# Two graph-attention layers on 64 graphs: layer 1's values from seven half-size products instead of eight matmuls

## The chip, the cores and the metric

The kernel runs on one core of a Trainium2 chip. The metric is the device time of one execution in microseconds (us); the kernel before took 3634.82 us in the median of three runs (3634.51 to 3635.04). Engines are named as in the profile: PE is TensorE's matmul and PEld its weight load, DVE is VectorE, ACT is ScalarE, POOL is GpSimd, SP is SyncE, which here only issues DMAs.

## What is computed

There are 64 graphs of 256 nodes with 512 features, float32, and a 256 x 256 adjacency (bool) for each. Two layers follow each other, each as a residual on a normalised input:

```python
h = jnp.maximum(_layernorm(x, axis=-1), 0.0)
x = x + layer0(h, adj, ...)     # 8 heads of 64: cosine adjacency times softmax attention, then a graph convolution
h = jnp.maximum(_layernorm(x, axis=-1), 0.0)
x = x + layer1(h, adj, ...)
```

Layer 1 is masked attention with 4 heads of 64:

```python
q = split_heads(x @ Wq)          # Wq, Wk, Wv: 512 x 256
k = split_heads(x @ Wk)
v = split_heads(x @ Wv)
sim = jnp.einsum('bhid,bhjd->bhij', q, k) * scale
sim = jnp.where(adjacency_mask[:, None, :, :], sim, neg)
attn = jax.nn.softmax(sim, axis=-1)
out = jnp.einsum('bhij,bhjd->bhid', attn, v)
return out.transpose(0, 2, 1, 3).reshape(...) @ Wo + bo
```

The change is about `v = x @ Wv`, a product of 256 x 512 by 512 x 256 for each graph.

## The kernel before

The graphs go through a software pipeline. `period(i)` is called 63 times; in it, layer 0 of graph i ends, layer 0's projections of graph i + 1 are made, layer 1 of graph i starts (queries, keys, values) and layer 1 of graph i - 1 ends. `closing()` does the last graph. The whole runs in a manual schedule: each engine executes its instructions in the order in which the program text issues them, and semaphores are set by the tile framework where a tile is read, written or used again. So the order around the change is what `period` and `closing` write out by hand.

Most projections are made as a block product with seven instead of eight half-size products (a Strassen-like scheme). Of the left matrix (tokens by features, cut into four blocks a11, a12, a21, a22) `left_factors` (L257 to L260) makes four further factors s1 to s4 on POOL; of the weights, `load_seven` loads four blocks and `finish_seven` (L88 to L91) makes three more by differences on DVE, once. `seven_products` (L279 for features first, L274 for tokens first) is a generator: each `next` issues one step of products into PSUM banks, the copies of some of them on ACT (`u2`, `u4`, `u5`, L289 without a bias, L296 with one), and the sums on DVE that write the result (L304) or an intermediate (`uu`, L324). One bank, `z`, is written by three steps in turn, accumulating; between them DVE reads it. Several such generators run interleaved: `m` and `s` (layer 0's mapping and messages), `q` and `k` (its queries and keys), and `j`, layer 1's queries and keys in one (`queries_keys1`, with `wqk1`, where the first 256 features of the result are queries and the others keys).

Layer 1's values are not made so. `values_in` (L527) issues, for each half of the tokens, four matmuls with 128 x 128 of the normalised input `h1T` as weights and 256 columns of `Wv` moving, into one bank:

```python
nc.tensor.matmul(g.p_v[:, t, :], g.h1T[:, c, t * P:(t + 1) * P], w.wv1[:, c, :],
                 start=(c == 0), stop=(c == NKC - 1))
```

In `period` one half stands between the third and the fourth step of `j`, the other after it, and one DVE copy of 128 x 512 (L687) brings the bank to SBUF behind the `moments` (L197 to L200) of graph i + 3. In `closing` one half is split over the steps of `j` and the other comes after the scores, copied by ACT (L748).

The next period begins with layer 1's scores of this graph (L404, `sc<-qk`, weights of 64 rows), then layer 0's scores of the next (`sc<-qT,kT`), their exponentials on ACT (L411), and the masks on DVE (L418 with the edges of layer 1, L420 for layer 0), `units` (L387), and the halved sums of the masked exponentials on POOL (L424, later L460), on which the steps of `far_off` (L451, L454) depend.

PSUM is a ring of 8 banks, given out in turn (`bank`). SBUF tiles come from pools: `v`, `sms` (layer 0's head sums, written by `total`, L487) and `adb` (the complement of the adjacency as bf16, written on POOL by `edges`, L337, and read by the two transposing DMAs of L342, which make the mask of graph i + 2) have one buffer each. `gt` (a block-diagonal copy of `gcn_W`, L42 to L44) and `ident_b` are constants that live through the whole program; `gt` is used only in the first stage, where `fold` (L128) and `fold_bias` (L140) combine weights, and `ident_b` only in a general path that doesn't run with these inputs.

Of the kernel before, what the change touches and what calls it, by code (L numbers as in the profile page):

```python
# [8 lines left out]
F32 = mybir.dt.float32  # L9
BF16 = mybir.dt.bfloat16  # L10
# [19 lines left out]
class Weights:  # L30
# [4 lines left out]
    def __init__(self, nc, const, a):  # L35
        P, D, DH = 128, a["x"].shape[2], 64
        self.nc, self.const, self.a = nc, const, a
        self.ident = const.tile([P, P], F32, name="ident")
        make_identity(nc, self.ident)

        self.gt = const.tile([P, P], F32, name="gt")
        nc.vector.memset(self.gt, 0.0)  # L42
        for j in range(2):
            nc.gpsimd.dma_start(out=self.gt[j * DH:(j + 1) * DH, j * DH:(j + 1) * DH], in_=a["gcn_WT"])  # L44
        self.gb = const.tile([P, D // P], F32, name="gb")
        nc.gpsimd.dma_start(out=self.gb, in_=a["gcn_map_b"].rearrange("(c p) -> p c", p=P))
        self.ident_b = const.tile([P, P], BF16, name="ident_b")
        nc.vector.tensor_copy(self.ident_b, self.ident)
        self.below = const.tile([P, 1], F32, name="below")
        nc.vector.memset(self.below, -THRESHOLD)  # L50
        self.ones = const.tile([P, DH], F32, name="ones")
        nc.vector.memset(self.ones, 1.0)

        self.blk32 = const.tile([P, 32], F32, name="blk32")
        nc.vector.memset(self.blk32, 0.0)
        for j in range(2):
            nc.vector.memset(self.blk32[j * DH:(j + 1) * DH, j * 16:(j + 1) * 16], 1.0)

        self.two = const.tile([P, 2, 32], F32, name="two")
        nc.vector.memset(self.two, 0.0)  # L60
        for n in range(2):
            nc.vector.memset(self.two[:, n, n:n + 1], 1.0)
        self.wc = const.tile([P, 7, D // P // 2, D // 2], F32, name="wc")
        self.bc = const.tile([P, D], F32, name="bc")
# [7 lines left out]
    def load_seven(self, keys, name, queues=1):  # L72

        aps = [self.a[k] for k in (keys if isinstance(keys, tuple) else (keys, keys))]
        half = aps[0].shape[0] // 2
        t = self.const.tile([128, 7, half // 128, half], F32, name=name)
        for n, (i, j) in enumerate(self.BLOCKS):
            f = 0 if isinstance(keys, tuple) else j * half  # L80
            block = aps[j][i * half:(i + 1) * half, f:f + half]
            queue = (self.nc.sync, self.nc.scalar)[n % queues]
            queue.dma_start(out=t[:, n], in_=block.rearrange("(c p) f -> p c f", p=128))
        return t
# [21 lines left out]
    def load_rest(self):  # L106
        self.wv1 = self.load_w("Wv", "wv1")
        self.wqk1 = self.load_seven(("Wq", "Wk"), "wqk1")
# [11 lines left out]

    def fold(self, gws, bank, put, cs):

        nc, P = self.nc, 128
        NKC = self.gb.shape[1]
        for c in cs:
            p = bank(f"p_wc{c}", [P, NKC * P])
            for k in range(NKC):
                nc.tensor.matmul(p[:, k * P:(k + 1) * P], gws[k // 2][:, k % 2, c * P:(c + 1) * P], self.gt,  # L128
                                 start=True, stop=True)
            put(c, p)  # L130
# [3 lines left out]

    def fold_bias(self, gbb, bank):
        nc, P = self.nc, 128
        NKC = self.gb.shape[1]
        p = bank("p_bc", [P, NKC * P])
        for k in range(NKC):
            nc.tensor.matmul(p[:, k * P:(k + 1) * P], gbb[:, k, :], self.gt, start=True, stop=True)  # L140
        nc.scalar.copy(self.bc, p)
# [9 lines left out]
def fast_path(ctx, tc, a, w, chk, out):  # L151
# [41 lines left out]
    def moments(g, tag):  # L193
        st = small.tile([P, NT, 6], F32, tag="st", name=f"st{tag}")
        g.mv = small.tile([P, NT, 2], F32, tag="mv", name=f"mv{tag}")
# [136 lines left out]

    def edges(g):


        adb = sb1.tile([P, NT, S], BF16, tag="adb", name=f"adb{g.i}")
        nc.gpsimd.tensor_scalar(adb, g.ad, -1.0, 1.0, op0=ALU.mult, op1=ALU.add)  # L337
# [147 lines left out]
    def total(g, sm):  # L485
        g.sms = sb1.tile([P, S], F32, tag="sms", name=f"sms{g.i}")
        nc.scalar.activation(g.sms, sm, AF.Copy, accum_out=chk[:, g.i, 0:1])  # L487
# [4 lines left out]
    def sums_back(g):  # L492

        rt = bank(f"rt{g.i}", [P, NT, P])
        for t in range(NT):
            nc.tensor.transpose(rt[:, t, :], g.sms[:, t * P:(t + 1) * P], w.ident)  # L496
        r = small.tile([P, NT, 2, 4], F32, tag="r", name=f"r{g.i}", bufs=2)
        nc.vector.reciprocal(r, rt.rearrange("p t (k n) -> p t n k", n=32)[:, :, :2, :])  # L498
        rc = small.tile([P, NT, 2, 4], F32, tag="rc", name=f"rc{g.i}", bufs=2)
        nc.scalar.activation(rc, r, AF.Copy, accum_out=chk[:, g.i, 1:2])  # L500
        g.rk = small.tile([P, NT, H0], F32, tag="rk", name=f"rk{g.i}", bufs=2)
        for t in range(NT):
# [12 lines left out]
    def queries_keys1(g):  # L515

        left = left_factors(g.h1T, "sh", f"1_{g.i}")
        qk = sb1.tile([P, 2 * NIC, S], F32, tag="qk1", name=f"qk1_{g.i}")
        g.q1T, g.k1T = qk[:, :NIC, :], qk[:, NIC:, :]
        return seven_products(left, w.wqk1, None, qk, f"p_qk1{g.i}")  # L520

    def values_in(g, t, cs=range(NKC)):
        if t == 0 and cs[0] == 0:
            g.v = sb1.tile([P, NT, INNER], F32, tag="v", name=f"v{g.i}")
            g.p_v = bank(f"p_v{g.i}", [P, NT, INNER])
        for c in cs:
            nc.tensor.matmul(g.p_v[:, t, :], g.h1T[:, c, t * P:(t + 1) * P], w.wv1[:, c, :],  # L527
                             start=(c == 0), stop=(c == NKC - 1))

# [37 lines left out]
    def period(i):  # L567
# [83 lines left out]
        if n2:  # L651
            edges(n2)
        if b:
# [5 lines left out]
        if i == 0:  # L659
            w.finish_seven(w.wqk1)  # L660
        nc.scalar.activation(nx.rn, nx.rn, AF.Sqrt)

# [11 lines left out]
        next(k)  # L674
        next(j)
        nc.vector.reciprocal(nx.rn, nx.rn)
        spread(nx)
        next(j)
        next(j)
        values_in(g, 0)  # L680
        next(j)
        if n2:
            n2.left_h = left_factors(n2.hT, "sh", n2.i)
        if i + 3 < B:
            moments(graphs[i + 3], f"0_{i + 3}")
        values_in(g, 1)
        nc.vector.tensor_copy(g.v, g.p_v)  # L687

    def closing():
# [28 lines left out]
        if not b:  # L718
            w.finish_seven(w.wqk1)
        g.sms = sb1.tile([P, S], F32, tag="sms", name=f"sms{g.i}")  # L720
        nc.vector.tensor_add(g.sms, sums(g, lambda c: both(g.e[c]), "sm"), first)
# [16 lines left out]
        for t in range(NT):  # L738
            nc.gpsimd.tensor_add(g.xs[:, t, :], g.xs[:, t, :], w.bo_b)
        next(j)  # L740
        next(j)
        next(j)
        values_in(g, 0, (0, 1))
        next(j)
        values_in(g, 0, (2, 3))
        g.e1 = [exps(products(g.k1T, g.q1T, c, f"sc1_{g.i}_{c}"), f"1_{g.i}_{c}") for c in range(NIC)]
        values_in(g, 1)
        nc.scalar.copy(g.v, g.p_v)  # L748
        if b:
# [33 lines left out]
    with tc.manual_schedule():  # L783
# [4 lines left out]
        gws = [sb2.tile([P, 2, D], F32, tag="e", name=f"gw{k}", bufs=6) for k in range(2)]  # L788
        w.load_folded(gws)
        w.load_scores()  # L790
        graphs.update({n: load(n) for n in range(1, min(3, B))})
# [16 lines left out]
        next(m)  # L808
        w.fold(gws, bank, w.put_seven, (0, 1))
        w.finish_seven(w.wq)  # L810
        next(m)
        w.finish_seven(w.wk)
        next(m)
        w.fold(gws, bank, w.put_seven, (2, 3))
        next(m)
        halved(g)
        squares(g)
        w.fold_bias(gbb, bank)
        w.finish_seven(w.wc)
# [27 lines left out]
def general_path(ctx, tc, a, w, out):  # L847
# [16 lines left out]
    wc = one.tile([P, NKC, D], F32, tag="gwc", name="gwc")  # L864
    gws = [one.tile([P, 2, D], F32, tag=f"ggw{k}", name=f"ggw{k}") for k in range(2)]
    w.load_folded(gws)
    wk = one.tile([P, NKC, D], F32, tag="gwk", name="gwk")
    nc.sync.dma_start(out=wk, in_=a["k_wT"].rearrange("(c p) f -> p c f", p=P))
    wq1, wk1 = (one.tile([P, NKC, INNER], F32, tag=f"g{k}", name=f"g{k}") for k in ("Wq", "Wk"))
    for t, k in ((wq1, "Wq"), (wk1, "Wk")):  # L870
        nc.sync.dma_start(out=t, in_=a[k].rearrange("(c p) f -> p c f", p=P))
    two = ctx.enter_context(tc.tile_pool(name="gtwo", bufs=2))
    small = ctx.enter_context(tc.tile_pool(name="gsmall", bufs=4))
# [48 lines left out]
    def exp_scores(neg, qT, kT, t, c0, name, sums=None):  # L922
# [3 lines left out]
        for s in range(2):  # L926
            nc.tensor.matmul(sc[:, s], w.ident_b, neg[:, t:t + 1, :].to_broadcast([P, 2, S]),
                             start=True, stop=False)
# [32 lines left out]

    w.fold(gws, bank, lambda c, p: nc.vector.tensor_copy(wc[:, c, :], p), range(NKC))

    with tc.For_i(0, B) as b:
# [76 lines left out]
        for t in range(NT):  # L1041
            p = tokens_first(w.wv1, hT, t, f"gp_v{t}")
            nc.scalar.copy(v[:, t, :, :DH], p.rearrange("p (h d) -> p h d", d=DH))
# [98 lines left out]
```

## Time and profile before

| what | value |
|---|---|
| median of three runs | 3634.82 us |
| the profiled execution | 3633.84 us, of which the span of its instructions is 3632.1 us |
| PE clock granted | 0.999 of full |
| period of the steady state (first `sc<-qk` to the next) | 56.07 us, 63 periods, all but the ends alike to 0.01 us |
| matmuls of `p_v` (L527) | 1024 records, 379 ns each, 242.5 us busy |
| matmuls of `p_qk` and `p_qk_z` (L279) | 3584 records, 275 to 277 ns each |
| DVE copy `v<-p_v` (L687) | 63, 678 ns each |
| DVE operation on 128x256 from PSUM (L304) | 425 ns |
| ACT copy of 128x256 from PSUM (L289) | 373 ns |
| POOL factors (L257 to L260 for `sh`) | 730 ns each |

How to read it: a matmul in float32 leaves two records, and their ends are modelled, so two records that follow each other overlap; the distance between two starts is what one costs when PE is never idle. In a timeline row the first number is the start in us from the start of the span, the second the length of the whole group, then engine, line, operation, out<-in, shapes and the number of instructions; in brackets the idle time of that engine before it and what ended it. In a row of groups the two numbers after the bar are the busy time in us and the mean of one in ns, and after the second bar comes the idle time before. The chain is followed back from the last instruction to what released it, and gives each engine's share of the span.

### The profile page before, as it was taken

The page shows a single profiled execution, that of the slowest core. Times are in us where ns is not written, and L with a number is a line of the kernel's source. Part 1 is how long each engine was busy: PE and PEld are TensorE (multiplying, and loading weights), DVE is VectorE, ACT ScalarE, POOL GpSimd, SP SyncE. Part 2 cuts the span into 40 slices and gives each one's busy share as a digit, 9 for nine tenths or more (in the row PEclk, how much of TensorE's full clock was granted, in tenths as well). Part 3 has the DMA queues.
Part 4 walks back from the last instruction along what each step waited for, and adds up shares of the span by engine and source line. Part 5 has one row for each costly group of instructions (what it writes and reads, how often), then busy time and mean ns, then how long its engine had stood idle before and what let it go on. Part 6 is the DMA issues. An engine that isn't in the chain of part 4 may idle for free.

```text
span 3632.1 us, 76457 instructions
## 1 busy us (share of the span) xinstructions
PE 3608.6 (99%) x29177; PEld 3083.9 (85%) x29177; DVE 2677.7 (74%) x5289; ACT 1904.7 (52%) x4481; POOL 2221.8 (61%) x2044
## 2 busy tenths in 40 slices
PE   8999999999999999999999999999999999999998
PEld 7888888888888888888888888888888888888886
DVE  7777777777777777777777777777777777777776
ACT  4555555555555555545555555555555555555543
POOL 4656666566566665665656656656566566665662
PEclk9999999999999999999999999999999999999999
DMA  4121121111211212112121121121111211211111
GB/s 119 44 58 44 54 56 47 55 46 53 61 44 53 57 46 56 45 54 61 42 55 52 50 58 44 54 58 45 55 47 53 61 44 53 58 47 55 45 48 34
DMA packets 358633, 191.48 MB, mean 53 GB/s; under 512 B 270300, under 2 KB 324600, under 8 KB 358264
## 3 DMA queue, kind: packets, MB, share of 16 engines
q1 hardware_dynamic: 357528, 185.97, 19.1%
q8 instruction: 234, 3.83, 0.4%
q14 instruction: 135, 1.11, 0.1%
q10 hardware_dynamic: 544, 0.52, 0.0%
q0 software_dynamic: 192, 0.04, 0.0%
HBM read 94.41 MB, written 34.34 MB: 35 GB/s over the span
## 4 chain that ended last, share of the span: by engine, by line
PE 98%; DVE 1%; DMA 0%; ACT 0%; issue 0%; POOL 0%; SPq 0%; DVEq 0%; ACTq 0%; POOLq 0%
PE sc L404 9%; PE av L431 9%; PE p_q L279 7%; PE p_m L279 7%; PE p_k L279 7%; PE p_qk L279 6%; PE p_v L527 6%; PE p_s L274 6%; PE p_o L564 6%; PE co L441 5%; PE p_qk_z L279 5%; PE p_q_z L279 5%; PE p_m_z L279 5%; PE p_k_z L279 5%; PE p_s_z L274 5%; PE sm L481 2%
## 5 line engine op out<-in xcount | busy, mean ns | idle before, releaser
L424 POOL TENSOR_TENSOR d<-e 128x512 f32<-128x512 f32 x376 | 585.7, 1584 | 354.4 <-DVE e L420 354.4
L460 POOL TENSOR_TENSOR d<-d,e 128x512 f32<-128x512 f32 x504 | 635.6, 1282 | 170.9 <-DVE e L465 170.9
L411 ACT ACTIVATE e<-sc 128x512 f32<-128x512 f32 x768 | 383.4, 647 | 383.3 <-PE sc L404 377.0
L513 POOL TENSOR_TENSOR xs<-xs,o 128x512 f32<-128x512 f32 x128 | 188.8, 1498 | 354.8 <-DVE o L511 354.8
L257 POOL TENSOR_TENSOR sh<-hT 128x256 f32<-128x256 f32 x128 | 93.8, 733 | 473.5 <-ACT hT L220 283.5
L420 DVE TENSOR_TENSOR e<-e,mask 128x1024 f32<-128x1024 f32 x256 | 377.7, 1497 | 0.4 <-ACT e L411 0.4
L454 DVE SCALAR_TENSOR_TENSOR e<-co,e 128x256 f32<-128x256 f32 (+1 forms) x1024 | 287.7, 346 | 62.5 <-ACT up L451 35.6
L451 ACT ACTIVATE up<-co,below 128x128 bf16<-128x128 f32 x512 | 160.3, 365 | 182.5 <-PE co L441 177.1
L527 PE MATMUL p_v<-wv,hT 128*128 128x256 f32 x1024 | 242.5, 379 | 0.0
L431 PE MATMUL av<-e,sem 128*64 128x256 f32 x2048 | 232.4, 379 | 0.2 <-DVE e L465 0.2
L404 PE MATMUL sc<-qT,kT 64*128 64x256 f32 x2048 | 231.9, 376 | 0.0
L564 PE MATMUL p_o<-wo,own 128*128 128x512 f32 x512 | 230.7, 593 | 0.0
L404 PEld LDWEIGHTS sc<-qT,kT 64*128 64x128 f32 x2048 | 198.1, 187 | 23.3 <-ACT hT L220 0.3
L498 DVE RECIPROCAL r<-rt 128x16 f32<-128x16 f32 x64 | 16.5, 258 | 268.6 <-PE rt L496 268.6
L431 PEld LDWEIGHTS av<-e,sem 128*64 128x64 f32 x2048 | 146.7, 137 | 75.2 <-DVE e L465 1.1
L527 PEld LDWEIGHTS p_v<-wv,hT 128*128 128x128 f32 x1024 | 184.7, 190 | 20.1 <-issue 0.3
L234 ACT ACTIVATE xn<-xs,shift,rs 128x512 f32<-128x512 f32 x124 | 100.5, 810 | 193.0 <-POOL d L460 190.5
L197 DVE BATCH_NORM_STATS2 st<-xs 128x6 f32<-128x512 f32 x256 | 174.0, 680 | 26.8 <-POOL xs L513 23.3
L465 DVE SCALAR_TENSOR_TENSOR e<-far,e 128x256 f32<-128x256 bf16 x256 | 190.5, 763 | 0.6 <-DMA far<-up 0.6
L441 PE MATMUL co<-nT 64*128 64x256 f32 (+1 forms) x2048 | 185.0, 330 | 0.0
L441 PEld LDWEIGHTS co<-nT 64*128 64x128 f32 x2048 | 161.3, 187 | 19.5 <-issue 0.4
L564 PEld LDWEIGHTS p_o<-wo,own 128*128 128x128 f32 x512 | 92.4, 190 | 92.6 <-issue 91.2
(224 smaller groups left out, 9185.0 us busy)
## 6 DMA issues: line engine op xcount, KB each, us to landing
xs<-in_x_dram SPq DMA_DIRECT2D x64, 512.0 KB
nT<-by_rn SPq DMA_DIRECT2D x128, 256.0 KB
out_dram<-xs SPq DMA_DIRECT2D x63, 512.0 KB
own<-by_rz SPq DMA_DIRECT2D x126, 128.0 KB
ad<-in_adj_dram SPq DMA_DIRECT2D x64, 64.0 KB
far<-up SPq DMA_TRANSPOSE x256
turn<-flat SPq DMA_TRANSPOSE x248
mask<-adb SPq DMA_TRANSPOSE x128
```

The lines of the kernel that those rows point to most:

```text
L274: nc.tensor.matmul(region, src[:, c, :], wt[:, block, c, :], start=p not in opened, stop=True, skip_group_check=True)
L279: nc.tensor.matmul(region[:, f, :], wt[:, block, c, f * P:(f + 1) * P], src[:, c, :], start=p not in opened, stop=True, skip_group_check=True)
L404: nc.tensor.matmul(ps[s][:, j, :], rows[h, c, j * P:(j + 1) * P], cols[h, c, :], start=True, stop=True)
L411: nc.scalar.activation(e[:, s, :], p.rearrange("p j q -> p (j q)"), AF.Exp, scale=SCALE)
L420: nc.vector.tensor_mul(e, e, m)
L424: nc.gpsimd.tensor_add(d, e[:, :, :S], e[:, :, S:])
L431: nc.tensor.matmul(av[s * DH:(s + 1) * DH, n, :], vs[:, j, (h0 + s) * DH:(h0 + s + 1) * DH], q[:, s, j * S:(j + 1) * S], start=(j == 0), s ...
L441: nc.tensor.matmul(ps[s][:, j, j * P:], g.nT[h, c, j * P:(j + 1) * P], g.nT[h, c, j * P:], start=(j == 0), stop=True, skip_group_check=True)
L454: nc.vector.scalar_tensor_tensor(e, p.rearrange("p j q -> p (j q)")[:, lo:hi], THRESHOLD, e, op0=ALU.is_gt, op1=ALU.mult)
L460: nc.gpsimd.tensor_add(g.d[c], g.d[c], g.e[c][:, :, half * S:(half + 1) * S])
L527: nc.tensor.matmul(g.p_v[:, t, :], g.h1T[:, c, t * P:(t + 1) * P], w.wv1[:, c, :], start=(c == 0), stop=(c == NKC - 1))
L564: nc.tensor.matmul(p, b.avs1[:, c, t * P:(t + 1) * P], w.wo1[:, c, :], start=(c == 0), stop=(c == NIC - 1))
```

## The change

`values_in` becomes a generator of four steps that makes the values by seven products of 128 x 128 blocks. It takes the left factors that `queries_keys1` has made for `j`, now kept in `g.left`; `Wv` is loaded as four blocks and finished by `finish_seven`, once. Each product is two matmuls (four records) with 128 columns moving. Three products are copied by ACT (`u2`, `u5`, `u4` of 128 x 128), and five DVE operations of 128 x 128 (four results and one intermediate) read PSUM in place of the one copy. In `period` and `closing` the steps alternate with those of `j`: j v j v j v j v, and nothing of the values comes after the last.

`sms` and `adb` no longer have buffers of their own: both lie in a tile of the tag `v`, so that head sums, the adjacency's complement and the values follow each other in one buffer. (In `closing` the head sums take a buffer of the tag `d`.) `gt` moves into a buffer of the exponentials, `ident_b` into the general path, and `st`, `r`, `rc`, `rk` have fewer buffers.

```diff
 def load_seven(self, keys, name, queues=1):
-        t = self.const.tile([128, 7, half // 128, half], F32, name=name)
+        width = aps[0].shape[1] if isinstance(keys, tuple) else aps[0].shape[1] // 2
+        t = self.const.tile([128, 7, half // 128, width], F32, name=name)
...
 def load_rest(self):
-        self.wv1 = self.load_w("Wv", "wv1")
+        self.wv1 = self.load_seven("Wv", "wv1")
...
+    def both_homes(i):
+        return sb1.tile([P, NT, S], F32, tag="v", name=f"homes{i}")
+
+    def edges(g, home=None):
-        adb = sb1.tile([P, NT, S], BF16, tag="adb", name=f"adb{g.i}")
+        adb = (both_homes(g.i) if home is None else home)[:, 1, :].bitcast(BF16).rearrange("p (t q) -> p t q", q=S)
...
     def total(g, sm):
-        g.sms = sb1.tile([P, S], F32, tag="sms", name=f"sms{g.i}")
+        g.homes = both_homes(g.i)
+        g.sms = g.homes[:, 0, :]
...
     def queries_keys1(g):
-        left = left_factors(g.h1T, "sh", f"1_{g.i}")
+        g.left = left_factors(g.h1T, "sh", f"1_{g.i}")
...
-    def values_in(g, t, cs=range(NKC)):
-        if t == 0 and cs[0] == 0:
-            g.v = sb1.tile([P, NT, INNER], F32, tag="v", name=f"v{g.i}")
-            g.p_v = bank(f"p_v{g.i}", [P, NT, INNER])
-        for c in cs:
-            nc.tensor.matmul(g.p_v[:, t, :], g.h1T[:, c, t * P:(t + 1) * P], w.wv1[:, c, :],
-                             start=(c == 0), stop=(c == NKC - 1))
+    def values_in(g):
+        a11, a12, a21, a22, s1, s2, s3, s4 = g.left
+        HI = INNER // 2
+        g.v = sb1.tile([P, NT, INNER], F32, tag="v", name=f"v{g.i}")
+        opened = set()
+
+        def product(p, region, block, src):
+            for c in range(HC):
+                nc.tensor.matmul(region, src[:, c, :], w.wv1[:, block, c, :], start=p not in opened, stop=True,
+                                 skip_group_check=True)
+                opened.add(p)
+
+        def copied(region, what):
+            t = sb2.tile([P, HI], F32, tag=f"u{what}", name=f"u{what}v{g.i}")
+            nc.scalar.copy(t, region)
+            return t
+
+        def out(t, f, x, y):
+            nc.vector.tensor_add(g.v[:, t, HI * f:HI * (f + 1)], x, y)
+
+        p24 = bank(f"p_v{g.i}_24", [P, 2, HI])
+        product("24", p24[:, 0], 1, a12)
+        p2 = copied(p24[:, 0], 2)
+        yield
+        pz = bank(f"p_v{g.i}_z", [P, HI])
+        product("z", pz, 0, a11)
+        out(0, 0, pz, p2)
+        p53 = bank(f"p_v{g.i}_53", [P, 2, HI])
+        product("53", p53[:, 0], 3, s1)
+        p5 = copied(p53[:, 0], 5)
+        yield
+        product("z", pz, 4, s2)
+        u4 = sb1.tile([P, HI], F32, tag="uu", name=f"uuv{g.i}")
+        nc.vector.tensor_add(u4, pz, p5)
+        product("53", p53[:, 1], 2, s4)
+        out(0, 1, p53[:, 1], u4)
+        yield
+        product("z", pz, 5, s3)
+        product("24", p24[:, 1], 6, a22)
+        p4 = copied(p24[:, 1], 4)
+        out(1, 1, pz, p5)
+        out(1, 0, pz, p4)
+        yield
...
 def period(i):
-            edges(n2)
+            edges(n2, g.homes)
...
             w.finish_seven(w.wqk1)
+            w.finish_seven(w.wv1)
...
         next(k)
         next(j)
+        v = values_in(g)
+        next(v)
         nc.vector.reciprocal(nx.rn, nx.rn)
         spread(nx)
-        next(j)
-        next(j)
-        values_in(g, 0)
-        next(j)
+        for step in (j, v, j, v, j, v):
+            next(step)
         if n2:
             n2.left_h = left_factors(n2.hT, "sh", n2.i)
         if i + 3 < B:
             moments(graphs[i + 3], f"0_{i + 3}")
-        values_in(g, 1)
-        nc.vector.tensor_copy(g.v, g.p_v)
...
 def closing():
-        next(j)
-        next(j)
-        next(j)
-        values_in(g, 0, (0, 1))
-        next(j)
-        values_in(g, 0, (2, 3))
+        v = values_in(g)
+        for step in (j, v, j, v, j, v, j, v):
+            next(step)
         g.e1 = [exps(products(g.k1T, g.q1T, c, f"sc1_{g.i}_{c}"), f"1_{g.i}_{c}") for c in range(NIC)]
-        values_in(g, 1)
-        nc.scalar.copy(g.v, g.p_v)
```

## The prediction

> **What bounds the kernel.** I read first the page (busy shares, chain that ended last), then the groups by shape, then the timeline of one middle period, engine by engine, and last the timeline of the end, where a wait is exposed that the middle hides.
>
> ```profile
> PE 3608.6 (99%) x29177; PEld 3083.9 (85%) x29177; DVE 2677.7 (74%) x5289; ACT 1904.7 (52%) x4481; POOL 2221.8 (61%) x2044
> ...
> PE 98%; DVE 1%; DMA 0%; ACT 0%; issue 0%; POOL 0%; SPq 0%; DVEq 0%; ACTq 0%; POOLq 0%
> ```
> TensorE is 98% of the chain: what shortens its stream shortens the kernel, and a wait of 0.1 us in a period, repeated 63 times, costs 6.3 us. Busy time alone doesn't say what a matmul costs, since records overlap; the spacing of starts does.
>
> ```profile
> L527 PE MATMUL p_v<-wv,hT 128*128 128x256 f32 x1024 | 242.5, 379 | 0.0
> ```
> Each matmul leaves two records (8 matmuls of p_v a graph, 64 graphs, x1024). Now the stage that changes, PE in the middle of the run:
>
> ```profile
> 1826.50 1.95 PE L279 MATMUL p_qk<-hT,wqk 128*128 128x128 f32 x16
> ...
> 1831.86 1.89 PE L527 MATMUL p_v<-wv,hT 128*128 128x256 f32 x8
> 1833.59 1.05 PE L279 MATMUL p_qk_z<-sh,wqk 128*128 128x128 f32 x8
> 1834.48 1.89 PE L527 MATMUL p_v<-wv,hT 128*128 128x256 f32 x8
> 1836.31 2.00 PE L404 MATMUL sc<-qk 64*128 64x256 f32 x16
> ```
> The reader is to see the differences of starts: 16 + 8 + 16 + 8 = 48 records of 128 columns (three rows left out) in 1831.86 - 1826.50 = 5.36 us, 0.1117 us each; 8 records of 256 columns in 1833.59 - 1831.86 = 1.73 us, 0.216 each. The second p_v block takes 1.83, 0.10 more: the scores after it use 64 rows, and that switch stays. No gap: PE never waits here.
>
> **Part 1, the products.** Values now: 16 records x 0.216 = 3.46 us a graph. After: seven products of 2 matmuls, 28 records of 128 columns, 28 x 0.1117 = 3.13 us. Saved: 0.33 us a period, 63 x 0.33 = 20.8 us. Arithmetic falls by 1/8, time by less (0.1117 is more than half of 0.216).
>
> A rule speaks against this. The Trainium skill ("TensorE: Matmul & The Clock Gate", Back-to-back issue gap) gives for streams that load weights before each matmul 81 ns at 128 columns and 131 at 512: small matmuls pay nearly as much as large ones. My interpolation for 256 columns is 98, so a 128-column matmul would cost 0.83 of a 256-column one, 28 x 0.83 x 0.216 = 5.0 us, 1.56 more than now, 98 us over the run. The rows decide: the same two shapes stand side by side in this stream, float32, and their ratio is 0.1117/0.216 = 0.52. I take the rows.
>
> **Part 2, the order and its waits.** Call the four steps of queries and keys j1 to j4 and of the values v1 to v4; the order becomes j1 v1 j2 v2 j3 v3 j4 v4, then scores. In records: 16, 4, 24, 8, 8, 8, 8, 8. Each step's second write to a shared bank waits for VectorE. From j3's end (time 0): j3's sum starts on DVE at 0.27 (1832.13 against 1831.86 now), its product at 0.73, the values' sum at 1.08, their product at about 1.35. j4 may start at 0.27 + 0.42 + 0.1 = 0.79; v3 covers it until 0.89. v4 may start near 1.4, covered until 1.78. These waits cost nothing; without v3 and j4 as cover they would cost up to 0.8 and 1.4.
>
> The wait that surfaces is the scores' for the last two writes of q and k. Now 1.83 us of p_v lie between; afterwards only v4, 8 x 0.1117 + 0.10 = 0.99 us. The end of the run shows this wait with such a short cover:
>
> ```profile
> 3608.98 1.03 PE L527 MATMUL p_v<-wv,hT 128*128 128x256 f32 x4
> ...
> 3609.18 0.42 DVE L304 TENSOR_TENSOR qk<-p_qk_z,u5p_qk 128x256 f32<-128x256 f32 x1 [0.80 <-PE p_qk_z L279]
> ...
> 3609.52 0.41 DVE L304 TENSOR_TENSOR qk<-p_qk_z,u4p_qk 128x256 f32<-128x256 f32 x1
> ...
> 3610.08 2.00 PE L404 MATMUL sc<-qk 64*128 64x256 f32 x16
> ```
> From j4's end (3608.98) two writes in turn, then the scores at 3610.08: 1.10 us. So scores start 1.10 - 0.99 = 0.11 to 0.12 late: I take 0.12, x63 = 7.6 us given back. It can't be below nothing; above, DVE could be held at that moment by the values' product, but by the sum above that one ends 0.3 us earlier. Ends: 0 and 0.2.
>
> **Part 3, DVE, ACT, POOL after it.** Queued behind the values' last write on DVE are the moments of a later graph and the masks:
>
> ```profile
> 1837.09 0.64 DVE L200 TENSOR_SCALAR rs<-mv 128x2 f32<-128x2 f32 x1
> 1837.64 0.68 DVE L687 COPY v<-p_v 128x512 f32<-128x512 f32 x1
> 1838.65 2.36 DVE L418 SCALAR_TENSOR_TENSOR e<-mask,e 128x1024 f32<-128x1024 bf16 x2 [0.34 <-ACT e L411]
> ```
> Removed: the 0.68 copy. Added: five 128x128 operations from PSUM; the nearest row is far_off's 128x128 form (L454, 278 ns, 0.20 from start to start): about 1.0 to 1.4 us. ACT gets three 128x128 copies; 128x256 takes 0.37 and 128x512 0.59, so about 0.27 each. ACT is idle up to 2 us between such copies: nothing, but the last is needed by the values' last write: v4 ends 0.99 - 0.10 = 0.89 after j4, copy at 1.1 to 1.4, write 1.45 to 1.65. With the scores at 1.10, moments start 0.55 after the scores (now 0.95 before), take 1.7 to `rs`, at 2.3, which waits for GpSimd's factors (now 0.64 instead of 0.17). Masks start at about 2.55 after the scores; now 2.34, set by ACT. DVE is 0.2 us late. Two masks of e, two more and `units` follow, GpSimd's sums wait behind them, then far_off, the shift, ACT's normalisation and the bias of the queries:
>
> ```profile
> 1860.98 0.62 ACT L296 ACTIVATE u5p_q<-p_q,bq 128x128 f32<-128x128 f32 x2
> ...
> 1861.92 0.43 DVE L324 TENSOR_TENSOR uup_q<-p_q_z,u5p_q 128x256 f32<-128x256 f32 x1
> ...
> 1862.46 1.10 PE L279 MATMUL p_q_z<-sm,wq 128*128 128x128 f32 x8
> ```
> ACT's bias ends at 1861.60 and DVE starts at 1861.92 (set by PE's product), so after about 0.05 for the signal some 0.25 us are spare; PE's last query group, which waits for that DVE sum, has none. A lateness of 0.2 costs nothing; every tenth above 0.25 costs PE a tenth. Ends: 0 and 0.45 us a period; I take 0, nearest to the sum. GpSimd's next factors (L257) start over an us later, but wait 5.7 us before the next sums: nothing.
>
> **Part 4, the shared buffer.** The values' first write waits for the mask's transposes (SP, issued from 1822.02 to 1824.5 now) and for `keep`, with all of DVE behind it. In the loaded start the same pair, issued from 21.5, let GpSimd go at 29.50, 8.0 us later; so landed by 1830.0 here, and the first write is due near 1832.2. Head sums wait for reads of the old values that are long past. Nothing, from 0 to 0.3. Fewer buffers for `st`, `r`, `rk` lie between operations a period apart: nothing. The moved `gt` DMAs queue behind one bias on POOL, under 1 us later; its first use is at 13.51, now landed near 9: nothing. Wv in four DMAs instead of one moves what follows on SP by about 1.3 us, the first masks (needed at 47) included: nothing.
>
> **Part 5, the two ends.** Wv's four differences (half of 0.69 each) add about 1.5 us to DVE once, ahead of key writes: 0 to 2, I take 0.5. At the end all values come before the scores: these start 1.4 us later, but the p_v block after them (1.83 us on PE) is gone and the masks then bound: 0.4 gained.
>
> **Sum**, against the profiled execution (3633.84; span 3632.1 and 1.7 around it): -20.8 + 7.6 + 0.5 - 0.4 = -13.1, so 3620.7. The median is 1.0 above that execution: 3621.7.
>
> **Rivals.**
> A, the forecast: products pay, scores wait 0.12. 3621.7, chance 0.60.
> B, the scores' wait stays hidden (DVE answers faster): 3633.8 - 20.8 + 0.1 + 1.0 = 3614.1. For: only 0.11 is missing; against: the end of the run shows it. 0.19.
> C, DVE's extra work eats the 0.25 spare and costs PE 0.15 more at the queries: + 9.5, 3631.2. For: 1.4 instead of 1.0 us of additions would do it. 0.14.
> D, slower: the same chain (values' writes, moments, masks, GpSimd's sums, shift, bias, fourth query step) late by 0.7 us, so PE loses 0.45 where it had gained 0.21: + 63 x 0.45 = 28.4, 3650. It decides from a lateness of 0.25 + 0.21 = 0.46. For: DVE and GpSimd hold each other up (L227: 1.19 us for two elements). Against: DVE idles 1.17 us before the next period's first write of m. 0.07.
>
> That the change doesn't do what it says is out: the instruction order shows 14 matmuls in place of 8.
>
> **Numbers.** 3621.7; 3613 to 3629 holds A, B and the near part of C. A measurement here can tell about 0.2% (7.3 us) from no change: under 3627.5 is faster (A, B, a little of C: 0.83), up to 3642 the same (0.10), above slower (0.07).
>
> **What will show it.** p_v records spaced 0.11 (if 0.13 or more, part 1 is wrong); scores 1.10 after j4's end (0.99: B); first query-step wait unchanged at PE (C and D: a gap before p_q_z's last group, masks over 0.25 later against the scores); no DVE wait on a DMA at the values' first write (part 4). A period of 56.07 now should read 55.86.

## The result and the profile after

The changed kernel takes 3623.74 us in the median of six runs (3623.55 to 3624.64); the kernel before, beside it, 3634.89 (3633.56 to 3635.12). The ratio is 0.997, with a 95% interval of 0.9957 to 0.9983. The prediction was 3621.7. The profiled execution took 3623.55 us, with a span of 3621.8 and a granted clock of 0.999; the prediction's sum for it was 3620.7, so 2.85 us are to be explained.

The page of the changed kernel has the same shape as before:

```profile
PE 3592.9 (99%) x29945; PEld 3131.8 (86%) x29945; DVE 2692.6 (74%) x5549; ACT 1942.8 (54%) x4672; POOL 2228.8 (62%) x2044
...
PE 97%; DVE 1%; DMA 1%; issue 0%; ACT 0%; POOL 0%; SPq 0%; DVEq 0%; ACTq 0%; POOLq 0%
```

TensorE still carries the chain. It has 768 more records and is busy for less time; VectorE has 260 more instructions and its share stays at 74%. So shares tell nothing here, and the stage has to be read. The timeline of PE in a middle period (first column the start, second the length of the group):

```profile
1829.79 1.06 PE L279 MATMUL p_qk_z<-sh,wqk 128*128 128x128 f32 x8
1830.68 0.61 PE L537 MATMUL p_v_z<-wv,sh 128*128 128x128 f32 x4
1831.13 0.61 PE L537 MATMUL p_v<-wv,hT 128*128 128x128 f32 x4
1831.79 2.00 PE L408 MATMUL sc<-qk 64*128 64x256 f32 x16
```

Four records of p_v take 1831.13 - 1830.68 = 0.45 us, 0.112 each. The last four should take that and 0.09 for the switch to 64 rows, and the scores should start at 1831.67; they start at 1831.79, so they wait 0.12. That is 1.11 after j4's end (1830.68). VectorE at the same time:

```profile
1830.89 0.42 DVE L304 TENSOR_TENSOR qk<-p_qk_z,u5p_qk 128x256 f32<-128x256 f32 x1
1831.23 0.41 DVE L304 TENSOR_TENSOR qk<-p_qk_z,u4p_qk 128x256 f32<-128x256 f32 x1
...
1832.08 0.29 DVE L547 TENSOR_TENSOR v<-p_v_z,u4v 128x128 f32<-128x128 f32 x1 [0.24 <-ACT u4v L543]
...
1834.01 0.36 DVE L200 TENSOR_SCALAR rs<-mv 128x2 f32<-128x2 f32 x1
1834.29 2.35 DVE L422 SCALAR_TENSOR_TENSOR e<-mask,e 128x1024 f32<-128x1024 bf16 x2
```

The second write of q and k ends at 1831.64, and the scores follow 0.15 later. The masks begin 2.50 us after the scores; before it was 2.34. In 55 of the 61 inner periods the distance from scores to scores is 55.86 us, as predicted, against 56.07 before.

Of the other six, one is 0.02 us longer and five are 0.23 to 0.43 us longer, 1.6 us in all; before, no inner period was. In four of the five, an instruction on VectorE or ScalarE starts 0.3 to 0.4 us late, and PE's wait for what hangs on it breaks through. In the fifth, the second graph's, VectorE waits 0.41 us for a DMA, and its operation then takes 1.79 us instead of 1.06. One of the four, where the sum before j4 starts 0.37 late and j4, due at 2723.59, comes 0.23 late (VectorE's row and PE's):

```profile
2723.34 0.42 DVE L324 TENSOR_TENSOR uup_qk<-p_qk_z,u5p_qk 128x256 f32<-128x256 f32 x1 [1.33 <-PE p_v_z L537]
...
2723.82 1.16 PE L279 MATMUL p_qk_z<-sh,wqk 128*128 128x128 f32 x8
```

The start of the run is slower too. The first scores come at 99.03 us (before 97.99), because VectorE makes the differences of `Wv` there, and PE waits for what stands behind them. The timelines of VectorE and of PE:

```profile
88.40 0.94 DVE L82 TENSOR_TENSOR wv<-wv 128x256 f32<-128x256 f32 x1
...
91.11 1.38 DVE L85 TENSOR_TENSOR wv<-wv 128x256 f32<-128x256 f32 x1
```

```profile
95.14 1.16 PE L279 MATMUL p_qk_z<-sh,wqk 128*128 128x128 f32 x8 [1.37 <-DVE qk L304]
```

The four differences last 4.1 us (88.40 to 92.49), not the 1.5 of the prediction: GpSimd makes its factors and adds a bias at the same time.

### The profile page after: what moved, and what is told of

It reads as the page before. It is cut to its first block, busy times and chain, and to the rows that moved or that the text cites. A ratio compares the mean times of both kernels' runs of the same rounds, so it can differ in the third digit from the quotient of the medians.

```text
span 3621.8 us, 79023 instructions
## 1 busy us (share of the span) xinstructions
PE 3592.9 (99%) x29945; PEld 3131.8 (86%) x29945; DVE 2692.6 (74%) x5549; ACT 1942.8 (54%) x4672; POOL 2228.8 (62%) x2044
## 4 chain that ended last, share of the span: by engine, by line
PE 97%; DVE 1%; DMA 1%; issue 0%; ACT 0%; POOL 0%; SPq 0%; DVEq 0%; ACTq 0%; POOLq 0%
PE sc L408 10%; PE av L435 9%; PE p_q L279 7%; PE p_m L279 7%; PE p_k L279 6%; PE p_qk L279 6%; PE p_s L274 6%; PE p_o L607 6%; PE co L445 5%; PE p_qk_z L279 5%; PE p_m_z L279 5%; PE p_q_z L279 5%; PE p_k_z L279 5%; PE p_s_z L274 5%; PE p_v L537 3%; PE p_v_z L537 2%
## 5 line engine op out<-in xcount | busy, mean ns | idle before, releaser
L424 DVE TENSOR_TENSOR e<-e,mask 128x1024 f32<-128x1024 f32 x256 | 361.0, 1430 | 0.5 <-ACT e L415 0.5
L408 PEld LDWEIGHTS sc<-qT,kT 64*128 64x128 f32 x2048 | 220.6, 187 | 1.1 <-ACT hT L220 0.3
L245 ACT COPY hT<-turn 128x1024 uint16<-128x1024 uint16 x124 | 167.5, 1351 | 0.0
L717 POOL TENSOR_TENSOR xs<-xs,bo_b 128x512 f32<-128x512 f32 x126 | 157.8, 1274 | 0.0
```

The source lines that it names most:

```text
L408: nc.tensor.matmul(ps[s][:, j, :], rows[h, c, j * P:(j + 1) * P], cols[h, c, :], start=True, stop=True)
L424: nc.vector.tensor_mul(e, e, m)
```

## The experiments

Theory 1 is the prediction's. A record's cost is what the spacing of starts shows; the alternation covers all waits of the eight steps but the scores', which is 0.12 a period; VectorE's further work stays just inside the spare at the fourth query step; the shared buffer is free. Each experiment attacks one of these.

**1. One matmul's price.** The kernel before, its eight products of the values issued in 128 columns:

```diff
-            nc.tensor.matmul(g.p_v[:, t, :], g.h1T[:, c, t * P:(t + 1) * P], w.wv1[:, c, :],
-                             start=(c == 0), stop=(c == NKC - 1))
+            for f in range(2):
+                q = slice(f * P, (f + 1) * P)
+                nc.tensor.matmul(g.p_v[:, t, q], g.h1T[:, c, t * P:(t + 1) * P], w.wv1[:, c, q],
+                                 start=(c == 0 and f == 0), stop=True, skip_group_check=True)
```

> The kernel before, with the eight products of the values split into matmuls of 128 columns: 32 records of 128 columns in place of 16 of 256, arithmetic unchanged. Theory 1 (a record of 128 columns costs 0.1117 us in this stream, 0.52 of one of 256): 32 x 0.1117 - 3.46 = +0.115 us a period, +7 us, 3642. By the back-to-back gap of the Trainium skill's page (TensorE: Matmul & The Clock Gate), a small matmul at 0.83 of one of 256 columns: 32 x 0.83 x 0.216 - 3.46 = +2.3 us a period, +143 us, 3778.

3642.31 us (3640.83 to 3643.11), ratio 1.0021 (1.0013 to 1.0029); the period is 56.19, 0.12 longer. PE's timeline in it:

```profile
1834.47 1.06 PE L279 MATMUL p_qk_z<-sh,wqk 128*128 128x128 f32 x8
1835.37 1.95 PE L529 MATMUL p_v<-wv,hT 128*128 128x128 f32 x16
1837.15 1.06 PE L279 MATMUL p_qk_z<-sh,wqk 128*128 128x128 f32 x8
```

Sixteen records of 128 columns take 1.78 us, 0.111 each. A pair of them costs 3% more than one of 256, so a product saved is almost wholly time saved. The back-to-back gap of the Trainium skill's page (TensorE: Matmul & The Clock Gate), as the expectation reads it, would have put this kernel at 3778.

**2. The scores' wait.** The kernel after, with a quarter of layer 0's scores ahead of layer 1's, and the masks in the order of their exponentials. These products need nothing of this stage; no work is added. (It is a quarter of layer 0's scores, 8 of 32 records, where the expectation says half.)

```diff
+        g.e[0] = exps(products(g.kT, g.qT, 0, f"sc0_{i}_0"), f"0_{i}_0")
         if b:
             b.e1 = [exps(products(b.k1T, b.q1T, c, f"sc1_{b.i}_{c}"), f"1_{b.i}_{c}") for c in range(NIC)]
-        for c in range(NKC):
+        for c in range(1, NKC):
             g.e[c] = exps(products(g.kT, g.qT, c, f"sc0_{i}_{c}"), f"0_{i}_{c}")
+        off_edges(0)
...
-        off_edges(0, 1)
+        off_edges(1)
```

> The kernel after, with the first half of layer 0's scores (about 0.93 us on PE, which need nothing of this stage) issued ahead of layer 1's scores, and the masks in the order of their exponentials. Theory 1 (layer 1's scores start 0.12 us late because they wait for the last two DVE writes of queries and keys, which v4 alone doesn't cover): the wait is gone in every period, -0.12 x 63 = -7.6 us, and the late starts of DVE that broke through in six periods at that place are covered too; about 3616 us, period 55.74. Rival (the 0.12 is a fixed cost of turning to 64 weight rows or of a PSUM bank, or what DVE and GpSimd do behind the scores is the true bound): no gain, 3623 to 3625, or slower if the masks come later.

3616.17 us (3615.52 to 3618.09), ratio to before 0.9951 (0.9938 to 0.9965). The period is 55.746, so 0.116 of the 0.12 came back. PE's timeline:

```profile
1827.30 0.61 PE L537 MATMUL p_v<-wv,hT 128*128 128x128 f32 x4
1827.84 1.13 PE L408 MATMUL sc<-qT,kT 64*128 64x256 f32 x8
1828.81 1.89 PE L408 MATMUL sc<-qk 64*128 64x256 f32 x16
```

Layer 0's scores start 0.54 after the last p_v block, with the same 64 rows: four records and the switch, no wait. A fixed cost of the switch or of the bank would have stayed. Three inner periods are longer, by 0.9 us together; in the changed kernel it was five (the expectation says six). In these three PE waits at the fourth query step (two) and at j4 (one), not at the scores, so this edit doesn't cover them.

The control is the same edit in the kernel before, where 1.83 us of products cover that wait:

> A control: the kernel before with the same order of scores and masks (layer 0's first scores ahead of layer 1's). In the kernel before 1.83 us of products cover the wait for the last writes of queries and keys, so theory 1 expects no gain: 3634.7 +- 1.5, period 56.07. Rival (the order itself is better for VectorE or GpSimd, whatever stands before the scores): about 7 us faster, 3627.

3634.62 us (3633.11 to 3636.31), ratio 0.9999 (0.9991 to 1.0008), period 56.07. The order by itself brings nothing; it repays the wait that the change opened.

**3. The alternation.** The kernel after, its value steps in one block (in `closing` they stay as they are):

```diff
-        for step in (j, v, j, v, j, v):
+        for step in (j, j, j, v, v, v, v):
             next(step)
```

(the first `next(v)` goes too.)

> The kernel after, with the four steps of the values in one block behind the four of queries and keys in each period (j j j j v v v v instead of j v j v j v j v). Theory 1 (each step's second write to the shared bank waits for DVE, and the other generator's step is the cover): j4 stands exposed for about 0.8 us after j3, v3 and v4 for about 0.2 each, while the scores' wait of 0.12 vanishes; about +1.1 us a period, 63 x 1.1 = 70, near 3693 us. Rival (the order doesn't matter, since DVE answers fast enough): 3616 to 3624.

3710.94 us (3710.03 to 3711.52), ratio to before 1.021 (1.0193 to 1.0227): 87 us slower than the change, with a period of 57.21, +1.35. PE's timeline:

```profile
1871.90 1.06 PE L279 MATMUL p_qk_z<-sh,wqk 128*128 128x128 f32 x8
1873.55 1.16 PE L279 MATMUL p_qk_z<-sh,wqk 128*128 128x128 f32 x8 [0.59 <-DVE uup_qk L324]
1874.54 0.61 PE L537 MATMUL p_v<-wv,hT 128*128 128x128 f32 x4
...
1875.44 0.61 PE L537 MATMUL p_v<-wv,sh 128*128 128x128 f32 x4
1876.14 0.71 PE L537 MATMUL p_v_z<-wv,sh 128*128 128x128 f32 x4
1876.68 0.61 PE L537 MATMUL p_v<-wv,sh 128*128 128x128 f32 x4
1877.29 0.71 PE L537 MATMUL p_v_z<-wv,sh 128*128 128x128 f32 x4
```

j4 comes 0.75 late (due at 1872.80), v3 0.25 late, v4 0.16: near the expected 0.8, 0.2, 0.2. What was not expected is that the group after each wait comes 0.09 to 0.10 late once more: j4's eight records take 0.99 instead of 0.89. That is three times 0.1 a period, and makes up most of the difference between the expected 70 us and the measured 87. It shows what the order j v j v is worth: without it the change would be a loss of 76 us.

**4. VectorE's spare.** The kernel after, its last write of the values repeated, two and four times more (same operands, same result):

```diff
         out(1, 0, pz, p4)
+        for _ in range(2):
+            out(1, 0, pz, p4)
         yield
```

> The kernel after, with the last DVE write of the values (128x128, same operands, same result) made three times instead of once: two more operations, about 0.4 us more on DVE in each period. Theory 1 (the masks are 0.16 us later against the scores than before, and of the 0.25 us spare at the fourth query step about 0.09 is left): 0.3 us a period reaches PE, +19 us, 3643. Rival (DVE at 74% busy has slack for this): no change, 3623 to 3625.

> The same with four more operations, about 0.8 us more on DVE in each period. Theory 1: 0.7 us a period reaches PE, +45 us, 3668; the slope between this and the run with two is one for one. Rival (DVE has slack): no change.

Two more: 3634.77 us (3633.16 to 3636.18), ratio 1.0 (0.9991 to 1.0008), period +0.18. Four more: 3680.87 (3680.17 to 3681.71), ratio 1.0127 (1.011 to 1.0144), period +0.94. So VectorE, 74% busy, has next to no slack, though the expected sizes, 0.3 and 0.7, were off both ways. The chain of the prediction's rivals C and D is in the timelines. In the changed kernel (scores at 1831.79):

```profile
1834.29 2.35 DVE L422 SCALAR_TENSOR_TENSOR e<-mask,e 128x1024 f32<-128x1024 bf16 x2
...
1850.97 1.27 POOL L428 TENSOR_TENSOR d<-e 128x512 f32<-128x512 f32 x1
...
1856.69 0.62 ACT L296 ACTIVATE u5p_q<-p_q,bq 128x128 f32<-128x128 f32 x2
...
1857.40 0.42 DVE L324 TENSOR_TENSOR uup_q<-p_q_z,u5p_q 128x256 f32<-128x256 f32 x1
```

With two more writes (scores at 1838.55):

```profile
1841.50 2.35 DVE L422 SCALAR_TENSOR_TENSOR e<-mask,e 128x1024 f32<-128x1024 bf16 x2
...
1857.98 1.26 POOL L428 TENSOR_TENSOR d<-e 128x512 f32<-128x512 f32 x1
...
1863.69 0.62 ACT L296 ACTIVATE u5p_q<-p_q,bq 128x128 f32<-128x128 f32 x2
...
1864.34 0.42 DVE L324 TENSOR_TENSOR uup_q<-p_q_z,u5p_q 128x256 f32<-128x256 f32 x1 [0.18 <-ACT u5p_q L296]
```

Counted from the scores, the masks go from 2.50 to 2.95, GpSimd's sum from 19.18 to 19.43, the bias from 24.90 to 25.14, and the DVE sum from 25.61 to 25.79, now with ScalarE's bias named as what it waits for. The two writes put 0.65 us on VectorE (0.33 each, where 0.2 was assumed); 0.19 of it goes because `rs` no longer waits for GpSimd's factors, and GpSimd's chain takes up another 0.2. Of the 0.24 that arrives at the bias, 0.18 reaches PE: the changed kernel had 0.06 us left. The two further writes come through in full: masks 0.65 later still, the period 0.76 longer, for PE then waits at a second place too (`p_s_z`).

**5. The shared buffer.** The kernel before with that part alone:

```diff
-        g.sms = sb1.tile([P, S], F32, tag="sms", name=f"sms{g.i}")
+        g.homes = both_homes(g.i)
+        g.sms = g.homes[:, 0, :]
...
-            edges(n2)
+            edges(n2, g.homes)
```

> The kernel before (values by eight products), with the shared buffer of head sums, adjacency complement and values alone. Theory 1 (the buffer costs nothing, since the transposes that read it have landed 2 us before the values' first write): 3634.8 +- 1. Rival (the shared buffer delays DVE or GpSimd and eats part of the gain of the products): 0.05 to 0.3 us a period, 3638 to 3654.

3634.99 us (3633.27 to 3636.12), ratio 1.0001 (0.9993 to 1.001), period 56.07. It costs nothing. (The fewer buffers of `st`, `r`, `rc`, `rk` and the moved `gt` were not run alone.)

**6. The start.** The kernel after, all eight differences of weights issued one stage earlier:

```diff
         if i == 0:
+            w.finish_seven(w.wqk1)
+            w.finish_seven(w.wv1)
...
         if i == 0:
-            w.finish_seven(w.wqk1)
-            w.finish_seven(w.wv1)
+            pass
```

> The kernel after, with the differences of the weights (wqk1 and wv1, once, before the first graph's layer 1) issued one stage earlier, where DVE is idle. Theory 1: the start of the run lost 1.04 us against the kernel before because DVE made these differences just ahead of the writes of layer 1's keys, and PE waited 1.37 us at the third step of queries and keys; moved, 1 to 2 us come back once and the periods stay at 55.86: about 3622. Rival (the first stage is bound by the loads of Wv in four pieces): no change, or slower if DVE then waits for Wv with other work behind it.

3623.82 us (3622.91 to 3624.93), ratio 0.9971 (0.996 to 0.9982): no gain. The time is the rival's, but VectorE waits for no DMA there. In the changed kernel VectorE is idle at that place for 4.95 us; here the eight differences take 6.2, the first two stretched beside GpSimd (1.42 and 1.64 us instead of 0.69). The row of the changed kernel, and then those of this one:

```profile
78.34 0.26 DVE L503 RECIPROCAL r<-rt 128x16 f32<-128x16 f32 x1 [4.95 <-PE rt L501]
```

```profile
73.47 1.42 DVE L82 TENSOR_TENSOR wqk<-wqk 128x512 f32<-128x512 f32 x1
...
79.65 0.25 DVE L503 RECIPROCAL r<-rt 128x16 f32<-128x16 f32 x1
```

The reciprocal comes 1.31 us later, and the transposes on PE start at 86.29 instead of 84.98. That is one part of the loss. The other stands on PE behind the transposes:

```profile
86.29 1.08 PE L219 MATMUL p_t<-ident,xn 128*128 128x128 f32 x8 [2.94 <-DVE xn L210]
87.21 1.81 PE L279 MATMUL p_k_z<-sm,wk 128*128 128x128 f32 x8
88.82 2.87 PE L279 MATMUL p_qk<-hT,wqk 128*128 128x128 f32 x16
91.52 0.61 PE L537 MATMUL p_v<-wv,hT 128*128 128x128 f32 x4
```

The 24 records from 87.21 to 91.52 take 4.31 us, 0.18 each, where 0.112 each would be 2.68. No wait stands there: the clock that PE was granted from 87.3 to 90.7 is 0.50, and in the changed kernel it is 1.00 in the same stretch. PE was idle for 2.94 us before the transposes, instead of 2.23. Together the two cost 2.9 us; the waits of 1.37 and of 0.77 (for `wqk`'s differences, in the kernel before too) are gone, each with the 0.1 behind it, and the first scores come at 99.58, 0.56 later than in the changed kernel. From this followed a version that moves only the four of `wqk1`, which fit:

> The kernel after, with only the four differences of wqk1 moved one stage earlier, those of wv1 where they were. Theory (they fit DVE's idle window of 4.95 us at the start): the first scores at about 97.5 to 98 us instead of 99.03, so 3622.3 to 3622.7; rival (the start is not bound by DVE): 3623.7.

3621.2 us (3620.05 to 3622.65), ratio 0.9963 (0.995 to 0.9977), first scores at 97.88: 2.5 us less than the changed kernel, 1.15 of it at the start of the run as expected. Both waits of PE are gone here as well; PE is idle for 2.24 us before the transposes, and its clock stays at 1.00. Of the rest, 0.4 is the second graph's period, which is not lengthened here, and 0.9 lies behind the last period's first scores, where the two kernels don't differ.

**7. Both kernels beaten.** The edit of experiment 2 with all differences earlier, then with those of `wqk1` alone:

> Both edits together (layer 0's first scores ahead of layer 1's, the differences of weights one stage earlier). If both causes hold and are independent: -7.6 - 1.5, about 3614.5 us, which would be faster than both kernels. If the scores' wait is not what costs 0.12 a period: about 3622.

> The kernel after, with layer 0's first scores ahead of layer 1's and only the four differences of wqk1 (not those of wv1) moved one stage earlier. Theory (at the start DVE has one idle window of 4.95 us, from 73.4 to 78.3; all eight differences took 6.2 us there and ran over it by 1.3 us, which came back as a later start of the transposes; wqk1's four take about 5 us at most and fit): the first scores come 1 to 1.5 us earlier than in the version with the scores' order alone, about 3615 us. Rival (what bounds the start is not DVE): no difference, 3616.2.

The first gave 3616.28 us (3615.49 to 3617.17), ratio 0.995 (0.9936 to 0.9964), as the scores' order alone: it misses its expectation by what experiment 6 shows, and its trace has the low clock too (0.50 from 86.6 to 90.0, after 2.94 us of idle time). So the expectation of the second version, which put the whole loss on the later transposes, gives only one of two reasons. The second gave 3614.68 us (3613.47 to 3615.85), ratio to before 0.9944 (0.993 to 0.9958). That is 20.0 us less than the kernel before, measured beside it; the change as it stands brought 11.2.

## Why the prediction was right

**Part 1** held: p_v records are spaced 0.112. The period without the scores' wait, in the version of experiment 2, is 55.746 against 56.075 before: 0.329 saved, where 0.33 was worked out. The skill's gap that spoke against it was off by a factor of 20 in the run made for it (2.3 us a period, 0.12 measured).

**Part 2** held to 0.01 us: 1.11 us from j4's end instead of 1.10, a wait of 0.12. The end of the old run, with its short cover, had shown this wait once; the change brought it into every period. The other half, that the remaining waits are covered, held as well; experiment 3 shows their price.

**Part 3** held in its result, zero, with both sides of its comparison a little too small. The masks are 0.16 later (predicted 0.2), but on the way through GpSimd's sums this grew to 0.24 at the bias. The spare was 0.29 us in the kernel before (the bias ended 0.32 ahead of the DVE sum, against 0.03 when it binds, in experiment 4), where 0.25 was read. So 0.06 was left. The two errors nearly cancel, which is luck: 0.24 against the 0.25 that was read would have left nothing. Rivals C and D were near; experiment 4 makes their case by hand.

**Part 4** held, shown for the shared buffer by experiment 5; VectorE's idle time before the values' first write, 1.89 us in the middle period, ends with PE's product and not with a DMA.

**Part 5** is mis-sized. The differences cost 1.0 us at the start (1.4 counted from the transposes, which in this trace come 0.38 earlier than before), not 0.5: the term "half of 0.69 each" left out GpSimd's work beside them, with which 0.42 (experiment 6, alone) became 0.83 to 1.38. At the end, from the first scores of the last period to the last instruction's end, +0.36 instead of -0.4. About 0.5 of it lies behind the last compute instruction; the time from the last `z` to the last VectorE instruction is the same in both traces (10.85 us). In the seven kernels here with the same closing code, the stretch from the last graph's layer 1 scores to the end varies from 20.11 to 21.09, so this half us can't be put on the change.

**What the sum lacked** is the longer periods, 1.6 us. With +0.5 at the start and +0.8 at the end this makes 2.9 of the 2.85 us missed; what else differs, in the periods' third decimal and in the last two periods, about cancels. A cover of 0.1 us was booked as cover; it is one only as long as no engine answers 0.3 us late, and sometimes one does. The median was missed by only 2.0 us by luck: the prediction added 1.0 for the distance of the median from the profiled execution, which in this kernel is 0.2.

Rival B, a hidden wait, was wrong by the trace. Its time (3614.1) is near what experiment 7 reaches when the wait is taken away and the start mended.

## What to carry to other kernels

Price a matmul by the spacing of starts of the same shape in the same stream, and a wait by the place in the old trace where the same chain stands with less cover. When a change shortens the work between two dependent steps, look for independent work to put there: here a reorder without new work gave 7.6 us, two thirds as much as the change. An engine at 74% can have 0.06 us to spare on the one chain that matters, so count from the event that starts the chain to the wait that ends it, not the share. When moved work brings less than the wait it removes, look at the granted clock of the stage before the whole loss is put on a moved delay: in experiment 6 the clock was 1.6 of 2.9 us.

## What the runs showed of the hardware that was not expected

An instruction on VectorE, ScalarE or GpSimd occasionally starts 0.2 to 0.4 us (in a few cases more) later than in the median period: about 25 times in some 59 periods of the changed kernel, 17 before, where PE's covers hid all of them. In 17 of these 42 a packet of an instruction queue (8 KB) begins 0.63 to 0.77 us after the late start; with some 140 such packets in 3600 us, chance would give 0.2 of 42. So these 17 go together with the loading of code, and the others may follow from such a start on another engine. The places go with the program too: the changed kernel and three of its versions (experiment 2, and those of 6 and 7 with `wqk1` alone) share three longer periods, the 9th, 31st and 47th, and the two with all differences earlier share the 9th, 27th and 58th. No run was made that changes the loading, so its cause stays open.

The first group behind a wait of PE that has 128 rows like those before it takes 0.09 to 0.10 us more (experiment 3). At the scores, whose change to 64 rows costs 0.09 with or without a wait, the wait of 0.12 cost only its length (0.116 came back in experiment 2). VectorE's 128x256 difference takes 0.42 us alone and 0.83 to 1.38 beside GpSimd's work.

PE's granted clock fell to 0.50 for one stretch of 3.41 us near the start in four traces: those of experiments 6 and 7 with all differences earlier (after 2.94 us of idle time), of experiment 3 (2.2 us after an idle time of 2.71) and of experiment 2's control (after 2.24). The other traces have 2.23 or 2.24 us of idle time at that place and a clock of 1.00. So the length of the idle time alone doesn't decide it; what else does was not tested.
